# The constant rows of the banded attention's operands: by transfers from one row in place of memsets

## The chip, the core and the metric

The kernel runs on one core of a Trainium2 chip. A core has five engines that run beside each other, each through its own list of instructions: TensorE (PE in the profile; its weight loads are PEld), VectorE (DVE), ScalarE (ACT), GpSimd (POOL) and SyncE (SP), which here only issues transfers (DMA). Sixteen DMA engines move the data. The metric is the device time of one execution in microseconds (us), the median of several executions.

## What is computed

The reference is a chain of four pairs of layers over `x` of 32 x 64 x 256 (2048 rows of 256) with a second input `ctx_2048` of the same shape; each layer adds to `x`:

```python
x = x + _L0_xattn_ref(_layernorm(x), ctx, ctx, gamma)          # A: attention, 8 heads
x = x + _L0_ffn_ref(_layernorm(x), ...)                        # B
x = x + _L1_xattn_ref(_layernorm(x), ctx, ...)                 # C
x = x + _L1_ffn_ref(_layernorm(x), ...)                        # D: attention, then 4 experts
x = x + _L2_xattn_ref(_layernorm(x), ctx, ..., 64)             # E: banded attention
x = x + _L2_ffn_ref(_layernorm(x), ...)                        # F: ternary weights
x = x + _L3_xattn_ref(_layernorm(x), ctx, ctx)                 # G
x = x + _L3_ffn_ref(_layernorm(x), ...)                        # H: 8 experts
```

The change concerns E, the banded attention, and is carried out beside D's experts:

```python
def _L2_xattn_ref(mask, encodings, w_in, b_in, w_out, b_out, w_ct, b_ct, local_size):
    ...
    scores = jnp.einsum('bqhd,bkhd->bhqk', q, k) / jnp.sqrt(jnp.asarray(d, q.dtype))
    band = jnp.abs(idx[:, None] - idx[None, :]) <= local_size
    scores = jnp.where(band[None, None], scores, neg)
    attn = jax.nn.softmax(scores, axis=-1)
    o = jnp.einsum('bhqk,bkhd->bqhd', attn, v).reshape(n, t, e)
    ...

def _moe(h, w_gate, we1, be1, we2, be2):
    raw = jax.nn.softmax(x @ w_gate, axis=-1)
    top_vals, top_idx = jax.lax.top_k(raw, TOP_K)
    ...
    hmid = jax.nn.gelu(jnp.einsum('td,edi->tei', x, we1) + be1[None], approximate=False)
    eout = jnp.einsum('tei,eid->ted', hmid, we2) + be2[None]
    out = jnp.einsum('te,ted->td', comb, eout)
```

## The kernel before

The 2048 rows lie in sixteen tiles of 128 rows. Eight stages A to H run one after another; most begin some of their work inside the stage before.

**Operands of the attention.** Stages A and E share `attention_slots`. A score is a product over a stack of rows: each float is split into three bf16 parts, and the parts of queries and keys are stacked so that one bf16 product has nearly the accuracy of float. For each tile there is a pair of stacks, `stk` and `stq`, of 128 rows x 16 heads x 256 columns in bf16, 8 KB a row. Rows 0 to 71 are written by transfers of 24 rows each (`stack_rows`, line 216) from DRAM, where `stacked` (line 208) has put the parts. Of the rest, `stk` needs ones (against rows 96 to 98 of `stq`, which receive the negated maximum in three parts through ScalarE's queue, line 267) and `stq` needs zeros. These are constants; they are written once into each of the four pairs that the tiles share in turn (`operand_buffers`, line 152) by a memset of rows 64 to 127, one for each of the two tensors. Rows 64 to 71 are then overwritten by `stack_rows`. The zero memset appears in the profile as 2048 elements of 32 bits, the one of ones as 4096 of 16.

**Where it runs.** Stage A calls `operand_buffers` at its own start. For E it is called from `first_of_E` (line 1282), a generator that `run_D_moe` (line 1175) advances in slots: the experts run sixteen steps (four groups of four tiles, four experts), and each step has three slots, `another()` (line 1233): before the two halves of its output, and after them. Slots go to `first_of_E` or to `ternary` (line 1372) by number: 0 to 3 and 8 to 11 to the first, 4 to 7 and 12 to 15 to the second, and so on. So the eight memsets stand in slots 0 to 3 and 8 to 11. The order of every engine's instructions there is the order of the program (`manual_schedule`).

**The experts.** For each step `hidden` (line 1187) makes the hidden products `hmp` (line 1194) and their GELU on ScalarE; `output` (line 1199) multiplies with `we2` into `ep` (line 1207, two buffers in PSUM), and VectorE adds each `ep`, weighted, to `h` (line 1210), which frees the buffer. After a group's four experts come the bias products `ebias` (line 1217, in the same two buffers). `routed_D` (line 971) works out the next group's routing in between: statistics (lines 86 to 91, the power on GpSimd), normalised rows `in_h` (line 95), logits, softmax and the two largest (lines 999 to 1020).

**The ternary weights.** `ternary` loads the three raw weight matrices of F, 1 MB each, one after another into one buffer `fw` (line 1382, on SyncE). Each is read by VectorE (line 1390) and ScalarE (line 1407); the next load waits for the latter.

After the constants and two tiles' operands have been prepared (`operands_of_E`), `run_E` takes over.

Of the kernel before, what the change touches and what calls it, by code (L numbers as in the profile page):

```python
# [10 lines left out]
BF = mybir.dt.bfloat16  # L11
# [6 lines left out]
P = 128  # L18
T = 2048
D = 256  # L20
# [11 lines left out]
def tile_net(ctx: ExitStack, tc: tile.TileContext, a: dict, out: bass.AP):  # L32
    nc = tc.nc
    V, S, G, PE = nc.vector, nc.scalar, nc.gpsimd, nc.tensor

    def bc(ap, axis, shape):
        return ap.unsqueeze(axis).to_broadcast(shape)
# [32 lines left out]
    def side_of(stage):  # L70
        return ("left", "right")[SEQ.index(stage) % 2]
# [77 lines left out]

    def operand_buffers(pool, k, b):

        pair = {}
        for kind, value in (("k", 1.0), ("q", 0.0)):
            pair[kind] = pool.tile([P, 16, D], BF, name=f"st{kind}{b}")
            V.memset(pair[kind][64:P], value)
            yield
        k.setdefault("st", []).append(pair)

    def attention_constants(pool, k):


        i3 = ident.rearrange("p (c m) -> p c m", m=32)
        k["shift"], k["mask"] = [], []
        for r in range(2):
            sh = pool.tile([P, 4, 32], F32, name=f"shift{r}")
            G.memset(sh, 0.0)
            G.tensor_copy(sh[:, :, 16 * r : 16 * r + 16], i3[:, :, 16 - 16 * r : 32 - 16 * r])
            k["shift"].append(sh.rearrange("p c m -> p (c m)"))  # L170
        yield
        k["vmo"] = []
        for b in range(2):
            vmo = pool.tile([P, 2, 4, 160], F32, name=f"vmo{b}")
            G.memset(vmo, 0.0)
            for lc in range(2):
                for q in range(4):
                    o = 32 * q + (8 * q + 16) % 32
                    G.memset(vmo[:, lc, :, o : o + 8], 1.0)
            k["vmo"].append(vmo)  # L180
        for r in range(2):
            m = pool.tile([P, 1], F32, name=f"mask{r}")
            V.tensor_reduce(m, k["shift"][1 - r], AX.X, ALU.add)
            k["mask"].append(m)
        yield
# [222 lines left out]
    def run_A(w, side):  # L408
        with ExitStack() as es:
# [8 lines left out]
            def prepare(i):  # L418
                if i + AHEAD < NT:
                    fetch(i + AHEAD)  # L420
                if i == 3:
                    pending.pop()()
                mv, rstd = ln_stats(pool, [xs[i]])
                V.tensor_scalar(mv[:, :, 0], mv[:, :, 0], -1.0, None, ALU.mult)  # L424
                yield
                q = pool.tile([P, D], F32, name="q")
                G.tensor_scalar(q, xs[i], mv[:, 0, 0:1], rstd, ALU.add, ALU.mult)
                if i < 4:
                    for _ in operand_buffers(cp, k, i):
                        pass  # L430
                yield
                yield
                yield
                yield from stacks(pool, k, dram, q, cs[i], i)
# [826 lines left out]
    def load_E(wp):  # L1261
        w = {}
        w["band"] = load(wp, [P, 2, D], a["c_band"], "band")
        for nm in ("b_in", "b_out", "b_ct"):
            w[nm] = load(wp, [P, 3 if nm == "b_in" else 1], a[f"L2_xattn_{nm}"], nm)
        bd = wp.tile([P, 5, P], F32, name="bd")
        G.memset(bd, 0.0)
        for h0 in (0, 64):
            rows = slice(h0, h0 + 64)
            nc.sync.dma_start(  # L1270
                bd[rows, 0:3, h0 : h0 + 64], a["L2_xattn_w_in"].rearrange("i (t o) -> i t o", t=3)
            )
            nc.sync.dma_start(bd[rows, 3, h0 : h0 + 64], a["L2_xattn_w_out"])
            nc.sync.dma_start(bd[rows, 4, h0 : h0 + 64], a["L2_xattn_w_ct"])
        w["bd"] = bd

        between.append(lambda psum: first_of_E(w, psum))
        return w
# [3 lines left out]
    def first_of_E(w, psum):  # L1282

        w["k"], w["cstack"], w["normed"] = {}, ExitStack(), {}
        side = side_of("E")
        cp = w["cstack"].enter_context(tc.tile_pool(name="Ec", bufs=1, side=side))
        for b in range(4):
            yield from operand_buffers(cp, w["k"], b)
        yield from attention_constants(cp, w["k"])

        bp = psum.tile([P, 1], F32, tag="tp", name="ebout")
        PE.matmul(bp, w["bd"][:, 3, :], w["b_in"][:, 2:3], start=True, stop=True)
        V.tensor_tensor(w["b_out"], w["b_out"], bp, ALU.add)
        w["bandb"] = cp.tile([P, 2, 2, D], BF, name="bandb")
        V.tensor_copy(w["bandb"], bc(w["band"], 2, [P, 2, 2, D]))
        w["dram"] = w["cstack"].enter_context(tc.tile_pool(name="Ed", bufs=4, space=bass.MemoryType.DRAM))
        yield
        xp = w["cstack"].enter_context(tc.tile_pool(name="Ex", bufs=4, side=side))
        w["xp"] = xp
        yield  # L1300
        with tc.tile_pool(name="Ef", bufs=1, side=side) as pool:
            for i in range(EARLY):
                yield from operands_of_E(w, pool, psum, i)

    def operands_of_E(w, pool, psum, i):
        ln = ln_stats(pool, [xs[i]])
        yield
        xn = w["normed"][i] = w["xp"].tile([P, D], F32, name="xn")
        ln_apply(xn, xs[i], *ln, 0)
        yield  # L1310
        fs = []
        for t, nm in ((0, "q"), (1, "k")):
            pp = psum.tile([P, D], F32, tag="tp", name=f"{nm}p_{i}")
            PE.matmul(pp, w["bd"][:, t, :], xn, start=True, stop=True)
            f = pool.tile([P, D], F32, name=f"f{nm}")
            S.activation(f, pp, AF.Identity, bias=w["b_in"][:, t : t + 1])
            fs.append(f)
            yield
        yield from stacks(pool, w["k"], w["dram"], fs[0], fs[1], i)
# [640 lines left out]
```

## Time and profile before

The median of three runs is 2780.76 us (2780.7 to 2781.12). The execution that the profiler recorded took 2783.1 us, of which the span from the first to the last instruction is 2781.4. The profile comes from that one execution; all its times count from the span's start.

| stretch, us | what runs | length | PE busy | VectorE busy | ScalarE busy | GpSimd busy | granted clock |
|---|---|---|---|---|---|---|---|
| 0 to 1300 | A to C, start of D | 1300 | 1058.0 | 1072.9 | 875.4 | 878.0 | 0.98 to 1.00 |
| 1300 to 1816 | D, attention | 516 | 514.7 | 271.2 | 274.0 | 272.9 | 1.00 |
| 1816 to 1879 | D, first experts | 63 | 48.6 | 41.6 | 19.0 | 5.9 | 0.86 |
| 1879 to 1976 | D, other experts | 97 | 95.1 | 52.7 | 38.8 | 27.3 | 0.98 |
| 1976 to 2286 | E | 310 | 269.5 | 208.8 | 151.4 | 234.3 | 0.99 |
| 2286 to 2781 | F, G, H | 495 | 446.2 | 229.8 | 173.0 | 115.5 | 0.87, then 1.00 |

The granted clock is the share of full speed that TensorE was allowed. In a row of the timeline come the start and length in us, the engine, the line of the code and the operation, then the tile written and the tiles read, the shape, and in brackets how long the engine had been idle before and what ended that. A bracket "<-issue" names no other engine: the engine waited for nothing that the profile shows. A row with x8 merges eight instructions. In the table of windows each row is a stretch of time with its length, then each engine's busy time (with the number of its instructions), the granted clock, the busy share of the DMA engines and the GB/s they moved.

### The profile page before, as it was taken

What the parts mean: (1) busy time and instruction counts of PE and PEld (TensorE: products, weight loads), DVE (VectorE), ACT (ScalarE), POOL (GpSimd) and SP (SyncE); (2) the same over time, 40 slices, a digit from 0 to 9 for tenths busy, and PEclk for the clock granted to TensorE, in tenths of its full rate; (3) what the DMA queues carried; (4) which work ended last, traced back from release to release, by engine and by line L of the source; (5) the groups of instructions that cost most, each with busy time, mean ns of one, the idle gap of its engine ahead of it and who ended that gap; (6) DMA issues with size and microseconds to landing.
All of it is one profiled execution on the core that took longest, in us unless ns stands there. A gap on an engine that the chain in (4) does not pass through costs nothing.

```text
span 2781.4 us, 44370 instructions
## 1 busy us (share of the span) xinstructions
PE 2432.0 (87%) x16078; PEld 1432.5 (52%) x16078; DVE 1876.9 (67%) x3919; ACT 1531.5 (55%) x2181; POOL 1533.9 (55%) x1764
## 2 busy tenths in 40 slices
PE   4999899778778778779999999979898887789999
PEld 2545344344444444446666666756555543456565
DVE  7888554899999999965454545666577758833232
ACT  1666321699999999846555555524255457831111
POOL 4665543588888888765555555503488765720000
PEclk9999999999999999989999999989999998989999
DMA  6553000699999999920000000001343412000000
GB/s 167 133 123 75 23 1 1 142 197 209 199 205 203 198 207 205 198 82 1 16 8 24 8 1 1 16 31 51 76 97 88 96 35 67 1 0 8 8 8 8
DMA packets 610599, 223.70 MB, mean 80 GB/s; under 512 B 547366, under 2 KB 600524, under 8 KB 605772
## 3 DMA queue, kind: packets, MB, share of 16 engines
q1 hardware_dynamic: 607308, 220.07, 36.1%
q8 instruction: 127, 2.08, 0.3%
q10 hardware_dynamic: 3072, 0.79, 0.2%
q14 instruction: 92, 0.75, 0.1%
HBM read 66.91 MB, written 18.87 MB: 31 GB/s over the span
## 4 chain that ended last, share of the span: by engine, by line
PE 47%; DVE 20%; issue 9%; POOL 5%; ACT 2%; DMA 1%; ACTq 0%; SPq 0%; POOLq 0%; DVEq 0%
DVE e L840 11%; PE yp L1137 4%; PE ppq L1078 4%; PE ppk L1078 4%; PE pgate L1836 4%; PE pup L1836 3%; PE hout L1812 3%; PE vp L1066 3%; PE sp L1096 2%; PE op L1122 2%; POOL e L291 2%; PE ep L1207 2%; PE hmp L1194 2%; PE sc L812 1%; PE op L801 1%
## 5 line engine op out<-in xcount | busy, mean ns | idle before, releaser
L864 ACT ACTIVATE ei<-e,nb,sq 128x2048 int16<-128x2048 f32 x256 | 535.4, 2092 | 39.7 <-DVE nb L861 36.2
L874 POOL CAST eb<-ei 128x2048 bf16<-128x2048 int16 x256 | 481.9, 1892 | 110.8 <-ACT ei L864 93.6
L812 PE MATMUL sc<-kT,qz 128*128 128x512 bf16 x1024 | 296.8, 380 | 142.0 <-DVE e L840 140.0
L251 DVE TENSOR_REDUCE negm<-s 128x2 f32<-128x512 f32 (+1 forms) x512 | 301.1, 611 | 125.7 <-PE s L247 122.4
L840 DVE TENSOR_SCALAR_CACHE_REDUCE e<-sc,mx 128x1024 f32<-128x1024 f32 x256 | 326.1, 1274 | 0.4 <-DVE nb L861 0.3
L840 DVE TENSOR_SCALAR_CACHE_REDUCE e<-sc 128x1024 f32<-128x1024 f32 x256 | 312.5, 1221 | 4.8 <-PE sc L812 4.8
L283 ACT ACTIVATE e<-s 128x1024 f32<-128x1024 f32 (+1 forms) x256 | 233.0, 915 | 148.7 <-PE s L279 110.6
L812 PEld LDWEIGHTS <-qz 128*128 128x128 bf16 x1024 | 94.5, 97 | 260.2 <-issue 202.6
L247 PE MATMUL s<-stk,stq 96*128 96x256 bf16 (+1 forms) x1024 | 191.6, 270 | 40.8 <-DMA d3k<-t3k 24.5
L1086 POOL TENSOR_TENSOR rwq<-rwq,sin 128x512 f32<-128x512 f32 x64 | 81.1, 1268 | 239.3 <-ACT rwq L1083 225.0
L279 PE MATMUL s<-stq,stk 128*128 128x256 bf16 (+1 forms) x1024 | 179.6, 261 | 8.7 <-DMA stq<-nm 5.0
L825 PEld LDWEIGHTS <-vz 128*64 128x64 bf16 x4096 | 123.3, 110 | 112.7 <-issue 112.3
L1846 DVE TENSOR_TENSOR hm<-pup,sl 128x512 f32<-128x512 f32 (+1 forms) x56 | 38.7, 691 | 200.5 <-PE pup L1836 193.6
L1098 DVE TENSOR_REDUCE mx<-sp 128x4 f32<-128x512 f32 x64 | 44.3, 692 | 190.6 <-PE sp L1096 190.6
L1083 ACT ACTIVATE rwq<-ppq,dbq 64x512 f32<-64x512 f32 x128 | 87.3, 682 | 153.7 <-DVE rtq L1080 150.2
L825 PE MATMUL av<-eT,vz 128*64 128x128 bf16 x4096 | 163.9, 223 | 5.9 <-DMA eT<-eb 5.8
L247 PEld LDWEIGHTS <-stq 96*128 96x128 bf16 x1024 | 93.5, 100 | 130.3 <-issue 107.5
L301 PE MATMUL o<-e,vmo 128*32 128x256 f32 (+1 forms) x2048 | 150.2, 365 | 7.2 <-POOL e L291 5.8
L291 POOL TENSOR_SCALAR_AFFINE_SELECT e<-e 128x256 f32<-128x256 f32 (+1 forms) x256 | 132.7, 545 | 31.2 <-ACT e L283 31.1
L1844 ACT ACTIVATE sl<-pgate 128x512 f32<-128x512 f32 (+1 forms) x56 | 33.4, 597 | 207.8 <-PE pgate L1836 207.8
L1066 PE MATMUL vp<-Dwv,hnT 128*128 128x512 f32 x256 | 122.1, 599 | 6.0 <-ACT hnT L945 5.5
L91 POOL TENSOR_TENSOR rstd<-ve,mhalf 128x1 f32<-128x1 f32 (+1 forms) x40 | 25.8, 646 | 182.8 <-DVE mv L424 69.2
(404 smaller groups left out, 5468.3 us busy)
## 6 DMA issues: line engine op xcount, KB each, us to landing
stk<-d3k SPq DMA_DIRECT2D x96, 192.0 KB
stq<-d3q SPq DMA_DIRECT2D x96, 192.0 KB
d3k<-t3k SPq DMA_DIRECT2D x160, 64.0 KB
d3q<-t3q SPq DMA_DIRECT2D x96, 64.0 KB
eT<-eb SPq DMA_TRANSPOSE x256
fw<-in_L_ffn_w SPq DMA_DIRECT2D x3, 1024.0 KB
x<-in_x SPq DMA_DIRECT2D x16, 128.0 KB
c<-in_ctx SPq DMA_DIRECT2D x16, 128.0 KB
```

What stands on the lines that cost most here:

```text
L247: PE.matmul(sc[:, hh, lo:hi], qs[0:96, 2 * hp + hh, qc * P : (qc + 1) * P], ks[0:96, 2 * hp + hh, lo:hi], start=band is None, stop=True, s ...
L251: V.tensor_reduce(negm[:, qc, 2 * hp : 2 * hp + 2], sc[:, :, lo:hi], AX.X, ALU.max, negate=True)
L283: S.activation(e[:, :, lo:hi], sc[:, :, lo:hi], AF.Exp, scale=scale)
L291: G.affine_select(e[:, :, s0:s1], e[:, :, s0:s1], [[0, 4], [step, s1 - s0]], ALU.is_ge, 0.0, base=base, channel_multiplier=chan,)
L812: PE.matmul(sc[:, k0 : k0 + 512], qz[i % 2][:, h, :], kT[:, h // 2, 1024 * part + k0 : 1024 * part + k0 + 512], start=True, stop=True,)
L825: PE.matmul(av[i][r0 : r0 + 64, h // 4, :], vz[:, kt, h // 4, h % 4, :], eT[:, kt, :], start=h == 0 and kt < 2, stop=h == H - 1 and kt >= ...
L840: V.tensor_scalar(e, scs.pop((n, part)), 1.0, mx[:, 0:1] if part else LOWEST, ALU.mult, ALU.max, accum_out=mx[:, part : part + 1],)
L864: S.activation(ei, es_.pop(n), AF.Exp, bias=nb, scale=sq[i][:, h : h + 1], accum_out=sums[i][:, h : h + 1],)
L874: G.tensor_copy(eb, eis.pop(n - 1))
L1066: PE.matmul(vp, hnT[g][:, c, j * P : (j + 1) * P], wv[:, c, :], start=c == 0, stop=c == 1)
L1078: PE.matmul(pp, wt[:, c, hh * P : (hh + 1) * P], hnT[g][:, c, :], start=c == 0, stop=c == 1)
L1836: PE.matmul(pp[:m], w[nm + "s"][:, c, cols], xnT[:, c, :], start=c == 0, stop=c == 1)
```

## The change

In `operand_buffers` a new argument `row` chooses between the memset and a transfer. `first_of_E` makes two tiles of 128 x 256 in bf16, fills one with ones and the other with zeros by a VectorE memset each, and passes them on. The transfer, issued by SyncE, reads rows 64 to 127 of such a tile sixteen times over and so writes the 16 heads of rows 64 to 127 of the operand. The caller in stage A passes no `row` and is unchanged. In `first_of_E` one `yield` is moved up, so that the pool of the normalised rows is opened a slot later.

```diff
-    def operand_buffers(pool, k, b):
+    def operand_buffers(pool, k, b, row=None):
 
         pair = {}
         for kind, value in (("k", 1.0), ("q", 0.0)):
             pair[kind] = pool.tile([P, 16, D], BF, name=f"st{kind}{b}")
-            V.memset(pair[kind][64:P], value)
+            if row is None:
+                V.memset(pair[kind][64:P], value)
+            else:
+
+                nc.sync.dma_start(pair[kind][64:P], bc(row[kind][64:P], 1, [64, 16, D]))
             yield
         k.setdefault("st", []).append(pair)
...
         cp = w["cstack"].enter_context(tc.tile_pool(name="Ec", bufs=1, side=side))
+        row = {}
+        for kind, value in (("k", 1.0), ("q", 0.0)):
+            row[kind] = cp.tile([P, D], BF, name=f"row{kind}")
+            V.memset(row[kind], value)
         for b in range(4):
-            yield from operand_buffers(cp, w["k"], b)
+            yield from operand_buffers(cp, w["k"], b, row)
         yield from attention_constants(cp, w["k"])
...
         yield
+        yield
         xp = w["cstack"].enter_context(tc.tile_pool(name="Ex", bufs=4, side=side))
         w["xp"] = xp
-        yield
         with tc.tile_pool(name="Ef", bufs=1, side=side) as pool:
```

## The prediction

> **What bounds the kernel now.** I read first the list of what line 157, the memset, did, because it is the only line whose instructions the change takes away:
>
> ```profile
> L157 DVE MEMSET stk<- x8: 3472/3472/3472, 4.7 to 1865.3; 64x4096 bf16 x8
> L157 DVE MEMSET stq<- x8: 1765/1765/1765, 8.9 to 1874.3; 64x2048 uint32 x8
> ```
>
> Sixteen memsets, in two places: stage A at the start, and the experts of stage D at 1817 to 1876 us. The diff passes `row` only in the second place, so eight go: 4 x 3.47 + 4 x 1.77 = 20.9 us of VectorE. VectorE is busy 67% of the span, so this alone says nothing of the time. I then read the timeline of 1815 to 1885 us, to see who is held up:
>
> ```profile
> 1829.07 0.88 DVE L1210 SCALAR_TENSOR_TENSOR h<-ep,comb,h 128x256 f32<-128x256 f32 x2
> ...
> 1832.42 1.02 POOL L91 TENSOR_TENSOR rstd<-ve,mhalf 128x4 f32<-128x4 f32 x1 [34.50 <-PE ep L1207]
> 1833.19 3.47 DVE L157 MEMSET stk<- 64x4096 bf16 x1 [0.91 <-issue]
> 1837.04 1.76 DVE L157 MEMSET stq<- 64x2048 uint32 x1 [0.37 <-issue]
> 1838.84 0.73 DVE L95 TENSOR_SCALAR in_h<-h,mv,rstd 128x256 f32<-128x256 f32 x2
> ...
> 1840.02 3.78 PE L1207 MATMUL ep<-we,hm 128*128 128x256 f32 x8 [6.87 <-DVE h L1210]
> ...
> 1864.09 3.60 PE L1207 MATMUL ep<-we,hm 128*128 128x256 f32 x8 [5.10 <-DVE h L1210]
> 1865.33 3.47 DVE L157 MEMSET stk<- 64x4096 bf16 x1 [0.91 <-issue]
> ...
> 1872.08 6.61 PE L1194 MATMUL hmp<-hT,we 128*128 128x512 f32 x8
> ```
>
> TensorE has two buffers for `ep`; line 1210 on VectorE empties them. Where a memset stands ahead of line 1210, TensorE stands still, 6.87 and 5.10 us in the two brackets. The chain that ended last agrees: of 1826 to 1873 us the memsets of `stk` are 22.2% and those of `stq` 11.3%. Last I read the windows of the same stretches, for the clock:
>
> ```profile
> core 0: us, PE busy (x) PEld busy (x) DVE busy (x) ACT busy (x) POOL busy (x), PEclk, DMA share, GB/s
> 1840.00:1844.00 4.00, 3.98 (x11) 3.15 (x12) 2.13 (x4) 0.00 (x0) 0.00 (x0) 0.52 0.00 0
> 1872.00:1879.00 7.00, 7.00 (x14) 3.02 (x14) 4.54 (x9) 2.25 (x3) 1.41 (x3) 0.57 0.00 0
> 1908.00:1912.00 4.00, 4.00 (x12) 1.94 (x12) 3.20 (x9) 0.59 (x2) 3.31 (x5) 1.00 0.00 0
> 1946.40:1949.80 3.40, 3.40 (x5) 1.34 (x5) 1.93 (x8) 0.00 (x0) 1.27 (x2) 0.52 0.02 5
> 1820.50:1851.50 31.00, 24.13 (x87) 15.81 (x88) 18.31 (x33) 8.90 (x14) 1.78 (x2) 0.89 0.01 1
> ```
>
> After the idle the granted clock is about half: eight `ep` matmuls take 3.78 and 3.60 us where a group at full clock takes 1.89. And the DMA engines are empty for 31 us (share 0.01).
>
> **The change part by part.**
>
> *Memsets with no cover lost, saving nothing.* The `stk` of 1817.2 runs while TensorE works on the first hidden products and ScalarE loads a table; VectorE then waits 4.76 us more for `ep`. The `stq` of 1874.3 ends at 1876.1 and VectorE waits 2.69 us at 1880.0.
>
> *First stall, `stq` at 1827.27, `stk` at 1833.19, `stq` at 1837.04.* Without the first, line 1210 empties the last two `ep` as they come, the second at 1828.0 to 1828.5 in place of 1829.95. The statistics behind it took 2.33 us, so they end at 1830.85; with 0.14 to GpSimd and 1.02 for `rstd`, the next VectorE work, line 95, starts at 1832.1 in place of 1838.84. GpSimd's `rstd` is what is late next. Before, TensorE followed 1.18 us after line 95; so 1833.28 in place of 1840.02: **6.74** saved, 0.13 of idle left. With the idle goes its half clock on this group: 3.78 - 1.89 = **1.89**.
>
> *Second stall, `stk` at 1855.05, `stq` at 1858.90.* They stand between the exponential of the routing and its fifteen small VectorE steps (2.96 us to line 1210). Without them (6.5 us with the gaps ahead of them) line 1210 could go at 1857.4 on the old scale, but its `ep` is only ready at 1858.0: TensorE's own work is late next, and it does not stop. **5.10**, and **1.71** of clock (3.60 - 1.89).
>
> *Third, `stk` at 1865.33.* It delays line 1210 to 1868.84, and TensorE's bias products start at 1869.38 where `ep` ended at 1867.69: **1.69**, and 0.2 as the four bias products then take 2.5 us like those of the next group.
>
> *The clock after the bias products.* [...] The eight `hmp` from 1872.08 took 6.54 us on the chain where eight take 3.44: 3.1 lost. [...] No gap of that size is left, so by the rule 3.1 is gained: sum 6.74 + 1.89 + 5.10 + 1.71 + 1.69 + 0.2 + 3.1 = **20.4**. But the row of 1946.40 has 0.52 with TensorE busy throughout, right after the bias products of a later group (which feed only 4 rows), and there eight `hmp` took 5.33: by that row 1.9 stays lost, **18.5**. The same place of the group between, 1908 to 1912, has 1.00. One of each: I take the middle, **19.5**, and keep both.
>
> *Added on VectorE:* two memsets of one row, 256 bf16 at 3472/4096 ns = 0.22 us and 128 words, like the `kp` memsets of line 617, 0.165 us. They stand where the first `stk` stood, under the same 4.76 us of waiting: nothing; without this cover 0.4.
>
> *Added on SyncE:* eight fills of 64 rows x 8 KB = 0.52 MB, read as 512-byte pieces. The trace has no such transfer. From below, the rows of the large weights, 401 GB/s: 1.3 us each. From above, the writes of `d3` in 512-byte pieces at 110 GB/s, held back by their own issue: 4.8 us. In between the stack traffic of 1934 to 1940 with 178 GB/s: 2.9 us, which I take, being part 512-byte too. [...] Issue on SyncE: the `hwgate` loads, also 1024 pieces, took 0.43 to 0.46 us each, up to 3 us with the queues full; SyncE has nothing else there.
>
> *Order on SyncE.* The first fill waits for the row memset (1817.5); behind it stand three fills and the second `fw` load, which itself waits for ScalarE until 1851.7 (1843 in the new run). The first `fw` is issued before all fills and has landed at 1820.2. Four fills end at about 1832; the second `fw` goes out at 1843 into empty queues and is read at about 1856; four more fills follow it and end at about 1859; the third `fw` goes out at 1869. The next to touch filled rows are the stack rows of line 216 (rows 48 to 71 overlap the fill) at about 1912, after them the three rows from ScalarE's queue, then the matmuls of E: all find the fills landed 50 us before. The moved `yield` issues nothing: the number of slots is the same, one pool opens one slot later.
>
> *Down to the end.* From 1879 on no memset stood in the way. The experts' end is TensorE work, E starts on its results (chain at 1974: bias product, line 1218, GpSimd's `x`, statistics), and later loads are released by that work too, so the 19.5 go through. The profiled execution: span 2781.4, itself 2783.1 with what lies around it. Median 2780.76; 2780.8 - 19.5 = **2761.3**.
>
> **Rivals.**
>
> *The idle goes, the half clock stays* (its windows fall otherwise). For it: the row of 1946.40. Against: the two slow `ep` groups each follow a real idle. Only 6.74 + 5.10 + 1.69 = 13.5 are won: **2767**.
>
> *The ternary loads come late*: the fills share the queues with the second `fw`, which has 13 us left between issue and use where it had 24. Three megabytes at 178 GB/s are 17.7 us, a stall of some 5: gain 15 and less, **2766 to 2770**. Against: it is issued first.
>
> *The stall is only passed on*, so that E starts no earlier: **2781**. For it speaks only that E begins with chains over all engines; against, that their first link is the experts' last product.
>
> *Slower: fills on one DMA engine.* If all eight go through one engine (401/16 = 25 GB/s, 21 us each), its share of the third `fw` lands at 1817.7 + 167 + 5 = 1990 where it is needed at 1879.5: 110 late, less 20, **2871**. It costs from 7 us a fill, and is slower than before from 9.6 us. For it: no transfer out of a repeated row is in the trace. [...]
>
> That the change doesn't do what it says: of sixteen memsets only the eight near stage E go; stage A's stay, and with them whatever they cost.
>
> **How the numbers follow.** Forecast 0.68 (own range 2759.5 to 2763); clock 0.14; late loads 0.06; passed on 0.05; slower 0.07. What can't be told from no change is 0.2%, 5.6 us. Faster 0.68 + 0.14 + 0.06 = 0.88, same 0.05, slower 0.07. The range takes in the clock and the late loads and a little beyond the 20.4, for windows that fall better later: 2757 to 2770.
>
> **What would show it.** No 64-row memset after 100 us; TensorE idle ahead of `ep` under 1 us in both brackets; clock 1.00 at the two `ep` groups; eight 0.5 MB transfers from 1818 to 1860, with line 1390 never waiting; the first E score at about 1957 in place of 1976.5. Wrong if line 1390 or line 216 waits for a fill, or if the clock after the gaps stays half.

## The result

The changed kernel takes 2766.16 us (median of 6 runs, 2761.02 to 2769.85) against 2780.94 of the kernel before in the runs beside it (6 runs, 2778.29 to 2786.86): ratio 0.9946, 95% interval 0.9932 to 0.996, so 11 to 19 us faster. A second set of runs of the same kernel gave 0.9934 (0.9919 to 0.9948). The forecast was 2761.3, its own range 2759.5 to 2763, the whole range 2757 to 2770.

The profiled execution has a span of 2768.1 us, 13.3 less than before. But it reached the first hidden product of D's experts at 1820.08 us where the one before reached it at 1816.31, through code that is the same in both. So I measure from that product. The distance to E's first score is 160.2 us before and 142.9 after: **17.3 us** in the place of the change, and from the score to the end there is no difference to speak of (804.9 and 805.1). ("First score" is the first product of the score tile `s`.) In the code after the change line 1207 is 1211, 1210 is 1214, 1194 is 1198 and 1390 is 1398.

The timeline after, rows as in the prediction:

```profile
1835.03 3.96 PE L1211 MATMUL ep<-we,hm 128*128 128x256 f32 x16
1835.81 0.74 DVE L95 TENSOR_SCALAR in_h<-h,mv,rstd 128x256 f32<-128x256 f32 x2 [1.19 <-POOL rstd L91]
...
1852.21 3.62 PE L1211 MATMUL ep<-we,hm 128*128 128x256 f32 x16
...
1855.76 2.79 PE L1221 MATMUL ebias<-be,dcT 4*128 4x256 f32 x8
...
1858.48 5.11 PE L1198 MATMUL hmp<-hT,we 128*128 128x512 f32 x8
```

The two groups of eight `ep` on either side of the old stall are now one row of sixteen, 3.96 us long where sixteen without a pause take 3.62: of 6.87 us of idle 0.34 are left, and VectorE waits for GpSimd's `rstd`, the next late thing. The second stall is gone altogether. What is left is the slow `hmp` behind the bias products, 5.11 us where eight take 3.68.

SyncE's timeline shows the first fills (start, length on the queue):

```profile
1819.60 0.37 SPq L1390 DMA_DIRECT2D fw<-in_L_ffn_w  x1
1820.49 0.66 SPq L161 DMA_DIRECT2D stk<-rowk  x1
1821.20 0.67 SPq L161 DMA_DIRECT2D stq<-rowq  x1
1821.91 4.12 SPq L161 DMA_DIRECT2D stk<-rowk  x1
```

Two issue freely, in 0.66 us; the third is held 4.1 us while the DMA engines are in full work (share 1.00 from 1822 to 1824), and nothing else waits on SyncE. The windows of the same stretch and of the slow `hmp`, in the prediction's columns:

```profile
1858.40:1863.40 5.00, 5.00 (x9) 2.10 (x9) 2.69 (x8) 1.44 (x2) 1.41 (x3) 0.70 1.09 163
1826.00:1834.00 8.00, 8.00 (x31) 5.07 (x30) 3.55 (x11) 2.25 (x4) 0.00 (x0) 1.00 1.17 177
1822.00:1824.00 2.00, 1.78 (x5) 0.47 (x3) 0.00 (x0) 1.85 (x2) 0.00 (x0) 1.00 1.00 389
```

(The DMA share adds up the time of all packets, so it can pass 1, as the 1.17 here.) From 1822 the raw weights load at 389 GB/s; then the fills run at 177, 0.52 MB in 2.95 us each. TensorE is busy all through them. The first row shows the clock behind the bias products: 0.70, with TensorE busy 5.00 of 5.00.

### The profile page after: what moved, and what is told of

Read it like the earlier page. It is cut to its first block, busy times and chain, and to the rows that moved or that the text cites. A ratio compares the mean times of both kernels' runs of the same rounds, so it can differ in the third digit from the quotient of the medians.

```text
span 2768.1 us, 44270 instructions
## 1 busy us (share of the span) xinstructions
PE 2414.7 (87%) x15971; PEld 1431.1 (52%) x16078; DVE 1856.7 (67%) x3913; ACT 1532.9 (55%) x2181; POOL 1534.5 (55%) x1764
## 4 chain that ended last, share of the span: by engine, by line
PE 47%; DVE 19%; issue 9%; POOL 6%; ACT 2%; DMA 1%; ACTq 0%; POOLq 0%; DVEq 0%
DVE e L844 11%; PE yp L1141 4%; PE ppq L1082 4%; PE ppk L1082 4%; PE pgate L1844 4%; PE pup L1844 4%; PE hout L1820 3%; PE vp L1070 3%; POOL e L295 2%; PE sp L1100 2%; PE op L1126 2%; PE hmp L1198 2%; PE ep L1211 2%; PE sc L816 1%; PE op L805 1%
## 5 line engine op out<-in xcount | busy, mean ns | idle before, releaser
L816 PE MATMUL sc<-kT,qz 128*128 128x512 bf16 x930 | 281.0, 381 | 154.6 <-DVE e L844 150.6
```

Source lines behind the costliest of these rows:

```text
L816: PE.matmul(sc[:, k0 : k0 + 512], qz[i % 2][:, h, :], kT[:, h // 2, 1024 * part + k0 : 1024 * part + k0 + 512], start=True, stop=True,)
```

## The experiments

All stretches are counted from the first hidden product of the experts. "Transposition" is that of group 1's routing weights, the first mark behind all the memsets.

| kernel | transposition | E's first score | first product reached at | median (runs) | before, same set (runs) |
|---|---|---|---|---|---|
| before | 62.2 | 160.2 | 1816.3 | 2780.94 (6) | |
| after | 43.3 | 142.9 | 1820.1 | 2766.16 (6) | 2780.94 (6) |
| after, again | 43.3 | 142.9 | 1820.4 | 2764.05 (6) | 2785.87 (11) |
| fills for buffers 0, 1 | 53.6 | 151.6 | 1816.7 | 2774.18 (1) | 2785.87 (11) |
| fills for buffers 2, 3 | 52.1 | 150.1 | 1813.3 | 2769.87 (1) | 2784.04 (1) |
| fills twice | 43.3 | 163.3 | 1816.3 | 2786.67 (1) | 2784.04 (1) |
| fills of 128 rows | 41.7 | 139.8 | 1811.3 | 2757.55 (1) | 2777.77 (1) |
| memsets on GpSimd | 50.9 | 150.5 | 1819.4 | 2773.54 (6) | 2785.87 (11) |
| the same in 32-bit words | 46.5 | 146.1 | 1821.6 | 2769.95 (1) | 2784.04 (1) |
| after, padded bias products | 41.8 | 137.8 | 1817.7 | 2759.92 (6) | 2785.87 (11) |
| before, padded bias products | 58.9 | 155.5 | 1817.6 | 2776.06 (1) | 2784.04 (1) |

A median is to be compared with the last column of its row, not with other rows: the kernel before alone differs by 8 us from set to set. The stretches are the finer measure. Between after and again they differ by 0.01 us; one fall of the clock behind the bias products more or less changes them by 1.4 to 1.7. From E's first score to the end the eleven profiles take 800.5 to 805.3 us.

**The kernel again.** No edit.

> The changed kernel unaltered, to set the size of the whole against the size in the place of the change. From the first hidden product of D's experts to E's first score the profile of before has 160.2 us, that of the changed kernel 142.9, so 17.3 less; the medians differ by only 14.8, and the profiled execution of the changed kernel reached that first product 3.8 us later than before, at code that the change does not touch. Theory A, run-to-run scatter: the stretch is again 17.3 us shorter than before, the first product is reached at some other time (1814 to 1821), and the ratio's interval holds 0.9938 (17.3 us). Theory B, something of the change costs 2 to 4 us upstream: the first product is again reached near 1820, and the ratio stays near 0.9946 or above.

The stretch is 142.89 us, and the first product came at 1820.36. That second number fits theory B, but the other runs speak against it: over the eleven profiles of the table the point is reached anywhere from 1811.3 to 1821.6 us, with code ahead of it that differs at most by the zeros of the padded kernels, and fills or none behind it. The ratio, 0.9934 (0.9919 to 0.9948), holds 0.9938. So the 3.8 us upstream are scatter between executions. The clock explains it in part at most: ahead of that point TensorE stood at half clock for 34 us in the earliest of the profiles (fills of 128 rows) and for 55 in the latest (memsets in 32-bit words), but the five with 48 us lie anywhere from 1813.3 to 1820.4. The rest is open.

**Half the fills.** The caller passes `row` for two buffers only; the other two keep their memsets:

```diff
-            yield from operand_buffers(cp, w["k"], b, row)
+            yield from operand_buffers(cp, w["k"], b, row if b < 2 else None)
```

> Fills for the buffers 0 and 1 only (slots 0 to 3); the buffers 2 and 3 (slots 8 to 11) keep VectorE's memsets. By the terms of the prediction only the first stall and its half clock go: 6.74 + 1.89 = 8.6 us, so the first group's end (the transposition of group 1's weights, 62.2 us after the first hidden product in before, 43.3 in the changed kernel) comes at about 53.6, the idle of 5.10 and 1.69 us ahead of expert and bias products remains. Rival, that the stalls are not additive and one exposes the other: later than 56 or earlier than 51.

And with `b >= 2`:

> Fills for the buffers 2 and 3 only (slots 8 to 11); the buffers 0 and 1 (slots 0 to 3) keep VectorE's memsets. The other half of the sum: the first stall stays (6.87 us of idle ahead of the expert products and their half clock), the second and third go with their clock: 5.10 + 1.71 + 1.69 = 8.5 us up to the first bias products (53.1 us after the first hidden product in before, 44.6 expected), and group 1's transposition at 62.2 - 8.5 - 1.5 = about 52.2 if the clock behind the bias products is half as in the changed kernel. With the 8.6 to 8.7 of the first half measured this makes the whole. Rival: the stalls are not additive and the bias products come later than 46 or earlier than 43.

The first half alone brings the transposition to 53.55 us, 8.66 earlier, for an expected 8.6. Its second stall is the old one to the hundredth:

```profile
1846.78 3.47 DVE L158 MEMSET stk<- 64x4096 bf16 x1 [0.91 <-issue]
...
1855.81 3.62 PE L1211 MATMUL ep<-we,hm 128*128 128x256 f32 x8 [5.10 <-DVE h L1214]
```

The second half alone puts the bias products at 44.4 (44.6 expected) and the transposition at 52.08, 10.13 earlier. 8.66 + 10.13 = 18.8, and the whole change has 62.21 - 43.34 = 18.9 at this mark. The stalls are additive, to 0.1 us.

**Every fill twice.**

```diff
-                nc.sync.dma_start(pair[kind][64:P], bc(row[kind][64:P], 1, [64, 16, D]))
+                for _ in range(2):
+                    nc.sync.dma_start(pair[kind][64:P], bc(row[kind][64:P], 1, [64, 16, D]))
```

> Every fill is issued twice into the same rows, the second waiting on SyncE for the first to land. This is the price at which the prediction lets the fills decide: from about 7 us a buffer they delay the loads of the raw ternary weights, from 9.6 us the kernel is slower than before. In the changed kernel four fills took 12 us, 2.95 each at 177 GB/s; two with a landing between make some 8 to 10 us a buffer, so SyncE is held until 1853 to 1861 in the first four (the second raw load left at 1847) and the third raw load leaves 10 to 25 us late. If the fills can decide, VectorE waits for that load (line 1398 in the changed kernel) by 5 to 15 us and the experts' stretch is 148 to 158 in place of 142.9. If they stay hidden for a reason the prediction does not have, the stretch stays at 143.

Each `stk` or `stq` now holds SyncE for 8.7 to 9.0 us (7.9 the first, 12.3 the one behind the second raw load), 9.2 on average. VectorE, whose line 1390 is line 1399 here, waits 5.3 us for the second raw load, which does not yet show in the stretch; the third leaves at 1891.0, and that wait does:

```profile
1899.79 2.34 DVE L1399 TENSOR_REDUCE wpart<-fw 128x1 f32<-128x1024 f32 x2 [16.99 <-DMA fw<-in_L_ffn_w]
```

All of the 17.3 is given back and 3.1 more: 163.3 us, longer than the expected 148 to 158 (17.0 of the 20.4 us against the changed kernel are this wait, and TensorE stands at half clock from 1891.7 to 1908.7). Up to the transposition nothing has changed (43.33). So the fills are free only because they end in time. The prediction let the change turn into a loss at 9.6 us a fill; at 9.2 it already is one.

**Fills of all 128 rows**, to see what holds them at 177 GB/s. Rows 0 to 71 are written over by the stack rows afterwards.

```diff
-                nc.sync.dma_start(pair[kind][64:P], bc(row[kind][64:P], 1, [64, 16, D]))
+                nc.sync.dma_start(pair[kind], bc(row[kind], 1, [P, 16, D]))
```

> Each fill writes all 128 rows of its operand from all 128 rows of the one-row tile, 1.05 MB in 2048 pieces of 512 bytes, in place of 64 rows and 0.52 MB; rows 0 to 71 are overwritten by the stack rows later, as before. In the changed kernel the fills ran at 177 GB/s with the DMA engines full (share 1.17), where the weight loads beside them reached 389. [...] Theory B, the short pieces set it: they stay near 180 GB/s and take 6 us each, eight take 47 us, the second four end near 1872 after the start at 1847 and the third raw load is not yet delayed much. [...]

The rate is 290 to 295 GB/s (DMA share 1.16 to 1.18), twice the bytes in 3.6 us in place of 2.95. Theory B, with 180 GB/s and 6 us each, does not hold as written: writing half the rows goes with about half of what is missing to the 389 of the loads (113 of 212 GB/s), and the other half remains. The short pieces, or the source in SBUF in place of DRAM, may be its cause; that was not separated. The stretch, 139.75, is shorter than the 142.9 of the narrow fills for another reason: here the hidden products behind groups 0 and 1 both ran at full clock (3.70 us), which is taken up below with the padded bias products. 160.21 - 139.75 = 20.5 is what the larger of the prediction's two sums gives.

**Memsets on GpSimd.** No transfers, and the two row tiles go with their memsets:

```diff
-                nc.sync.dma_start(pair[kind][64:P], bc(row[kind][64:P], 1, [64, 16, D]))
+                G.memset(pair[kind][64:P], value)
...
-            row[kind] = cp.tile([P, D], BF, name=f"row{kind}")
-            V.memset(row[kind], value)
+            row[kind] = None
```

> The eight memsets issued on GpSimd in the same slots, no rows and no transfers. If what was won is the relief of VectorE alone, and the fills cost nothing and bring nothing, the experts' stretch (first hidden product to E's first score) is 142.9 us, as with the fills, within the 1.5 us by which the clock after the bias products can fall either way, and the total is that of the changed kernel. Rival: GpSimd becomes what is late, since its power for the statistics, its casts of the ternary weights and its additions to x stand behind memsets of about 3.7 us (the 128x1280 float memset of the profile took 1.16 us, 0.9 ns an element): then TensorE waits at the expert products again and the stretch is 146 us or longer.

Nearly half of the gain is lost (150.5, so 7.6 of 17.3; ratio 0.9964, 0.9952 to 0.9977), but not as the rival had it. GpSimd is in time with its `rstd`; VectorE is held while GpSimd's memsets run:

```profile
1834.13 1.02 POOL L91 TENSOR_TENSOR rstd<-ve,mhalf 128x4 f32<-128x4 f32 x1 [8.08 <-DVE ve L89]
...
1835.19 7.28 DVE L95 TENSOR_SCALAR in_h<-h,mv,rstd 128x256 f32<-128x256 f32 x2 [1.21 <-POOL rstd L91]
1835.21 3.51 POOL L161 MEMSET stk<- 64x4096 bf16 x1
1838.66 3.65 POOL L161 MEMSET stq<- 64x4096 bf16 x1
...
1842.91 2.50 PE L1211 MATMUL ep<-we,hm 128*128 128x256 f32 x5 [6.62 <-DVE h L1214]
```

Two operations of line 95 take 7.28 us, where after the change they take 0.74, and end within 0.2 us of the two memsets; TensorE's 6.62 us of idle are back. The same with half the elements, the ones as the 32-bit word that holds two of them:

```diff
-                nc.sync.dma_start(pair[kind][64:P], bc(row[kind][64:P], 1, [64, 16, D]))
+                G.memset(pair[kind].bitcast(F32)[64:P], 1.0019378662109375 if value else 0.0)
```

> The memsets on GpSimd again, written as 2048 words of 32 bits in place of 4096 of 16 (the ones as the word that holds two of them). In the run with GpSimd memsets of 3.51 us two normalisations of VectorE (line 95) took 3.7 us each in place of 0.41 while the memsets ran, and TensorE waited 6.62 us for the additions behind them. [...] Theory B, VectorE waits for something else that GpSimd has done late in its queue: line 95 takes 0.41 us and its idle ahead of it is longer, or it stays at 3.7.

```profile
1837.40 3.86 DVE L95 TENSOR_SCALAR in_h<-h,mv,rstd 128x256 f32<-128x256 f32 x2 [1.21 <-POOL rstd L91]
1837.43 1.80 POOL L161 MEMSET stk<- 64x2048 f32 x1
...
1841.71 3.10 PE L1211 MATMUL ep<-we,hm 128*128 128x256 f32 x8 [3.21 <-DVE h L1214]
```

The stretched VectorE operations shrink with the memsets, 7.28 to 3.86, and TensorE's idle from 6.62 to 3.21, the stretch from 150.5 to 146.1. Theory B, with 0.41 us or 3.7 for one operation of line 95, does not fit: it takes 1.9. The runs show that the two operations last as long as the two memsets beside them; what holds them up they do not show. Not every VectorE operation was held: beside the 16-bit memsets of 1856.54 to 1866.95 the small steps of the routing took their 0.17 us and line 1214 its 0.48.

**Bias products over 128 rows.** The operands of `ebias` get 124 rows of zeros, written once:

```diff
-                combT = pool.tile([4, 512], F32, name="dcT", bufs=1)
-                S.copy(combT, tp[0:4].rearrange("e j t -> e (j t)"))
+                combT = w["dcT"]
+                S.copy(combT[0:4], tp[0:4].rearrange("e j t -> e (j t)"))
...
+            w["dcT"] = wpool.tile([P, 512], F32, name="dcT")
+            G.memset(w["dcT"], 0.0)
...
-                w["be2"] = load(hpool, [4, D], a["L1_ffn_be2"].rearrange("o e d -> (o e) d"), "be2")
+                w["be2"] = hpool.tile([P, D], F32, name="be2")
+                G.memset(w["be2"], 0.0)
+                nc.sync.dma_start(w["be2"][0:4], a["L1_ffn_be2"].rearrange("o e d -> (o e) d"))
```

> The changed kernel with the bias products of the experts fed from 128 rows instead of 4: 124 rows of zeros in both operands, the same count and shape of output, the zeros written once by GpSimd. In the changed kernel the eight hidden products behind the bias products of groups 0, 1 and 2 took 5.11, 5.40 and 5.40 us where eight at full clock take 3.68. Theory A, the clock goes down because a product over 4 rows counts as little work: with 128 rows all three take 3.7 us, the stretch falls from 142.9 to about 138 us, and the total falls by some 4.6 us against the changed kernel. Theory B, the clock goes down for the pauses of TensorE between the bias products (they wait for VectorE), or for where a window of the clock happens to end: the three stay at 5.1 to 5.4 or scatter, and the stretch stays at 142 to 144.

The stretch falls to 137.77, and the total to 2759.92 us, ratio to before 0.992 (0.9903 to 0.9937), beside 0.9934 for the unpadded kernel in the same set. The first group, line 1225 being the bias products and 1202 the hidden ones:

```profile
1853.52 2.65 PE L1225 MATMUL ebias<-be,dcT 128*128 128x256 f32 x8
...
1856.01 3.60 PE L1202 MATMUL hmp<-hT,we 128*128 128x512 f32 x8
```

The bias products take about the same time (2.65 us for 2.79), yet the clock does not fall: 3.60 us instead of 5.11. One such run could be chance, so the kernel before got the same edit:

> The kernel before, with its memsets on VectorE, and the bias products fed from 128 rows as in the run before this one. In before the hidden products behind the bias products took 6.61 (group 0, after real idle), 3.70 and 5.40 us. Theory A, four rows count as little work for the clock: groups 1 and 2 both take 3.7; group 0 keeps what its idle costs, between 3.7 and 5.4; so the stretch is 160.2 less 1.7 to 4.6, 155.6 to 158.5. Theory B, the end of a clock window happened to fall well in the padded kernel: group 1 or 2 takes 5 or more again.

All three groups are at 3.60 us here, and the stretch is 155.48, 4.7 less than before, 0.1 below what theory A allowed. Group 0, behind real idle:

```profile
1865.53 3.78 PE L1211 MATMUL ep<-we,hm 128*128 128x256 f32 x8 [5.10 <-DVE h L1214]
...
1873.06 3.60 PE L1198 MATMUL hmp<-hT,we 128*128 128x512 f32 x8
```

Behind the idle the next eight `ep` still take 3.78 us, where eight at full clock take 1.89. The clock is back at 1869.30, before the bias products begin at 1870.91; what differs is what follows them. The stretch of 3.41 us in which they stand and the one behind it, first in the kernel before, then in the padded one (the third number from the end is the granted clock):

```profile
1867.72:1871.13 3.41, 1.67 (x7) 1.04 (x8) 2.80 (x5) 0.00 (x0) 0.52 (x1) 1.00 0.00 0
1871.14:1877.96 6.82, 6.82 (x10) 2.82 (x10) 4.96 (x10) 1.97 (x2) 2.27 (x4) 0.50 0.00 0
1869.30:1872.71 3.41, 1.73 (x8) 1.16 (x8) 2.67 (x5) 0.00 (x0) 0.59 (x1) 1.00 0.00 0
1872.71:1876.12 3.41, 3.41 (x11) 1.68 (x11) 2.69 (x9) 1.10 (x1) 2.19 (x4) 1.00 0.00 0
```

TensorE is idle for half of that stretch in both (busy 1.67 and 1.73 us of 3.41). Behind 4 rows the clock then stands at 0.50 for 6.8 us, behind 128 rows it stays at 1.00.

**When the clock falls.** The traces answer what theory B asked. In each of the eleven, all changes of the granted clock lie on one grid with steps of 3.413 us, to within 0.002; in before, for one, the clock stood at 0.50 from 1837.0 to 1843.8, from 1864.3 to 1867.7 and from 1871.1 to 1878.0. The grid lies differently against the program in each execution. Two executions whose TensorE ran alike up to the bias products of group 0, after and the one with wide fills, cut along this grid:

```profile
1854.53:1857.94 3.41, 3.41 (x15) 1.90 (x13) 2.15 (x6) 0.28 (x2) 0.94 (x2) 1.00 1.20 179
1857.94:1861.35 3.41, 3.41 (x6) 1.33 (x5) 2.85 (x9) 0.00 (x0) 1.87 (x3) 0.50 1.19 177
1845.62:1849.03 3.41, 3.41 (x14) 1.94 (x13) 2.15 (x6) 0.35 (x2) 0.87 (x2) 1.00 1.17 290
1849.03:1852.44 3.41, 3.41 (x9) 1.48 (x9) 3.08 (x9) 0.97 (x1) 1.90 (x3) 1.00 1.16 290
```

The bias products begin 1.23 us behind a grid point in after and 1.31 behind one in wide: in the first the clock falls at the next point, in the second it does not. I counted a fall by the time from a group's bias products to the next transposition (5.6 to 6.4 us at full clock, 7.6 and more at half), and left out group 0 where idle stands right ahead. With 4 rows there are 25 cases. In the 18 that began at most 1.23 us behind a grid point, or at most 0.28 ahead of one, the clock fell; in the 7 that began 1.31 to 2.65 behind one it did not. So in these cases it fell where some 2.2 us of these products (an estimate: 3.41 - 1.23) lay within one step.

With 128 rows it fell in none of 6, but three of these (1.32, 1.94 and 2.59 us behind) stand where it did not fall with 4 rows either. Three tell: group 2 of both padded kernels (0.58 and 1.16), and group 0 above, 1.61 behind a grid point, where 4 rows brought the fall at 1.65 with the same idle ahead. The kernel before and its padded form lie nearly alike against the grid in all three groups (1.65, 2.18, 0.85 and 1.61, 2.59, 1.16), so these 4.7 us are the padding's. Of the 5.1 us between after and its padded form some 1.9, those of group 2, are surely so; groups 0 and 1 stood where the clock might have held without it.

## Why the prediction was right, and where its size was off

**The stalls.** Right to a few tenths. (The small steps ahead of line 1210 take 2.86 us in the rows, 1860.69 to 1863.55, not 2.96; nothing rests on it.) The first stall with its half clock was put at 6.74 + 1.89 = 8.63: the transposition of `in_h` behind it moved from 27.28 to 18.75 us, 8.53, and the first half alone gave 8.66. Up to the bias products the sum was 17.1; they moved from 53.07 to 35.68, 17.39. The next late things were those named: GpSimd's `rstd`, then TensorE itself.

**The cover.** The memsets of 1817 and 1874 us cost nothing before, as said: the sums above close without them, 17.1 expected up to the bias products and 17.39 measured. The row memsets (0.27 and 0.17 us) stand under 8.6 us of waiting.

**The fills.** 2.9 us each was taken from the stack traffic at 178 GB/s; 2.95 at 177 were measured. All landed by 1836 and 1864, line 1398 never waited, and the rival of late loads did not occur. Its threshold is real, as the doubled fills show.

**The clock after the bias products** is the term that was mis-sized. The forecast let it bring 2.2 us, the middle between the 3.1 of its larger sum and the 1.2 that the row of 1946.40 leaves. That the clock stays up as soon as the long idle is gone, on which the 3.1 rest, no run shows; what the runs showed at group 0 is 1.5 saved with the change (6.61 us became 5.11, near the row) and 2.9 with the wide fills (3.70). But I counted one group only. Group 1, at full clock before (3.70), went to 5.40: its bias products now began 0.28 us behind a grid point, where they had begun 2.18 behind one. That took 1.4 back: 18.9 saved at the transposition of group 1, 17.5 at that of group 2, 17.3 at E's first score, 2.2 short of 19.5. Idle alone does not account for it: behind products over 4 rows the clock fell in 18 of 25 cases, also with TensorE busy 3.41 of 3.41 us, and behind 128 rows of mostly zeros in none of 6. Which groups were hit went with the grid, which the prediction did not have and no edit here set: the kernel with wide fills has the full 20.5. The middle of two cases was a guess.

**The total.** By the medians the gain is 14.8, not 19.5. 2766.16 us lies outside the forecast's own range and inside the whole one only because that was drawn wider for a half clock that stays and for late loads, neither of which came; this part is luck. Of the 4.7 us that are missing the clock term is 2.2. The other 2.5 are of the size by which executions differ ahead of the change; the second set, with 18.4 by its ratio, does not miss them. E's first score came at 1963.0, not at 1957, for the same two reasons.

**Down to the end** the gain is kept: 804.9 us from the first score before, 805.1 after.

**The rivals.** The half clock did not stay at the two `ep` groups (sixteen in 3.96 and 3.62 us); the stall was not passed on to E; at 177 GB/s, with a share of 1.17 of sixteen DMA engines' time, the fills were not confined to one engine.

## What to carry to other kernels

An engine that is busy two thirds of the time can still be the bound of one stretch: look in the timeline for what stands in its queue ahead of the instruction that frees another engine's buffer, and take constants out of that queue, for a transfer was free there at 2.95 us a buffer, and no longer at 9.2, where a load that was needed stood behind it. Work moved from VectorE to GpSimd was not moved off VectorE's path, for two VectorE operations of 0.4 us took 3.6 beside GpSimd's memsets of 3.5: of the 17.3 us 9.7 were kept, and 14.1 with memsets of half the length. Where a TensorE stretch slows without idle, count the rows that its small products use; padding them here from 4 to 128 with zeros gained 4.7 us of 160.

## What the runs showed of the hardware

- The granted clock changed only at points 3.413 us apart, in all eleven traces. With bias products over 4 rows it fell in all 18 cases where they began at most 1.23 us behind such a point or 0.28 ahead, and in none of 7 that began 1.31 to 2.65 behind. With 128 rows it fell in none of 6, of which 3 stood where it fell with 4 rows.
- Beside a GpSimd memset VectorE's `tensor_scalar` of line 95 lasted as long as the memset: 3.6 to 3.7 us an operation beside memsets of 3.51 and 3.65 us, 1.9 beside 1.80 and 1.95, where it takes 0.41 alone.
- Transfers within SBUF in 512-byte pieces (2806 packets for 1.41 MB, 1826 to 1834 us of after) ran at 177 GB/s into 64 rows and at 290 into 128, where 4 KB rows from memory reached 389.
- A VectorE memset of 4096 elements is shown with 3.47 us, but in all four cases among the experts VectorE stood 0.91 to 0.95 us idle ahead of it, three times without a cause that the profile shows: it cost 4.4.
